# A macaron transformer block: load order, the last output tiles, and an order of steps for every sequence

## The chip, the core and the metric

The kernel runs on one core of one Trainium2 chip. The metric is the device time of one execution in microseconds (us). Before the change the median of three runs is 900.11 us (900.03 to 900.91).

The core has five engines that work side by side, each through its own list of instructions in order: TensorE (PE, with weight loads shown as PEld), VectorE (DVE), ScalarE (ACT), GpSimd (POOL) and SyncE (SP), which here only issues DMA transfers. An instruction waits until the semaphores of what it needs have been raised, and everything behind it on the same engine waits with it. Matmul results go to PSUM, from where VectorE or ScalarE carries them on.

## The reference

Eight sequences of 512 tokens with 256 features pass through half a feed-forward network, attention, and half a feed-forward network again; both feed-forward networks use the same weights.

```python
x = x + 0.5 * ffn(layernorm(x))
x = x + attn(layernorm(x))
x = x + 0.5 * ffn(layernorm(x))

def attn(x, Wq, Wk, Wv, Wo):                # 16 heads of 32 columns
    q, k, v = (heads(x @ W) for W in (Wq, Wk, Wv))
    scores = (q_r @ k_r.T + q_i @ k_i.T) / sqrt(16)
    probs = softmax(where(causal, scores, -inf))
    return concat(probs @ v_r, probs @ v_i) @ Wo

def ffn(x):                                 # 256 -> 1024 -> 256
    h = x @ W_exp + b_exp
    h = butterfly(h, up_weights)            # 10 stages of 2x2 mixing over 1024
    h = gelu(h + up_bias)
    h = butterfly(h, down_weights)
    return h @ W_con + b_con + down_bias
```

A butterfly is linear, so each can be multiplied into the dense matrix beside it once, before any token is touched.

## The kernel before

All arithmetic is in fp32. Matmuls are counted here as the trace shows them, two for each in the source.

**Prologue** (L613 to L632). The up butterfly is folded into W_exp, the down butterfly into W_con. The seven low stages of each are built as one 128x128 matrix per block of 128 features by VectorE (`low_matrices`, L223) and applied by TensorE (`low_up` L252, `low_down` L273). The three high stages pair whole blocks (`high_stage`): ScalarE scales a block (L236; for some of the down stages GpSimd, L238) and VectorE adds the partner (L241). `finish_up` transposes the result into `wup_sb` (L267, copied at L268). Small vectors are needed on the way: the stage coefficients `upc_sb` and `dnc_sb`, the bias `upb_sb`, and `bc_sb` and `db_sb`, which VectorE combines into `bhalf` (L616, L617). GpSimd adds `bhalf` to x (`ffn_bias`, L189). The first sequence's layer norm runs here too: its statistics on VectorE (L154 to L156), its normalization on GpSimd (L172), its transposes on TensorE (L195). `keep_busy` (L259) issues matmuls of the identity into a bank that nobody reads; each counts as two matmuls. The eight steps f of sequence 0 are spread over the down stages, and the statistics and normalization of sequence 1 end the prologue.

**Loads** (L117 to L135). SP and ScalarE each issue into a DMA queue of their own. The tables `upe_sb`, W_exp in two halves with x of sequence 0 between them, `dne_sb`, `wcon_sb`, further x and the attention weights go through SP; five small ones go through ScalarE's queue. A DMA also waits, if need be, until an earlier one on the same completion semaphore has landed; there are eight such semaphores, taken in turn.

**Sequences** (L634 to L636). What follows is one list of steps per sequence, written out as tokens in `ORDER` (L544) and turned into instructions by `sequence` (L573) in just that order: every engine gets its part of each step in the order of the tokens. A number ahead of a token repeats it; `+1`, `-1` and so on name another sequence, relative to the one whose list it is. Sequences 1 to 4 share one list (`None`), the others have their own. The tokens:

| token | step | work |
|---|---|---|
| f, g | `up_steps`, first and second feed-forward network | 4 matmuls of 512 columns (L307), GELU on ScalarE (L314); 8 steps |
| F, G | `down_steps` | 8 matmuls of 256 columns (L325); every fourth step VectorE adds into x (L334), G then stores (L336); 8 steps |
| q, v | `qk_steps`, `v_steps` | 4 matmuls of 512 columns (L350, L368), copy by ScalarE; 8 and 4 steps; q alternates q and k of a head group |
| u0 to u9 | `score_unit` | scores of 4 heads for one or two query blocks (L404) into the one 4-bank PSUM tile; VectorE adds the mask and takes the row maximum (L418), ScalarE exponentiates (L431) |
| t | `turn` | VectorE turns 32x32 blocks of the exponentials (L449, L453) |
| m | `turn_sums`, `move` | VectorE inverts and turns the sums (L458, L459), then SP issues 16 DMAs across partitions (L471) into the one tile `pt` |
| p | `times_v` | probs x V for a head group (L484), scaled by VectorE (L491) |
| w | `wo_steps` | 8 matmuls (L505), VectorE adds into x (L510) every second step |
| s, a, x | layer norm: `ln_stats`, `ln_apply`, `ln_steps`; second letter 1, a, 2 for the first network, attention, the second network | VectorE, rstd on GpSimd (L158), bias addition on GpSimd; x is a write to DRAM and a read back by DMA (L287, L294), which transposes; for three layer norms it is TensorE's transposes instead |
| l | `load_x` | loads x of a later sequence |

Units u0, u1 serve head group 0, u2 groups 0 and 1, u3, u4 group 1, u5, u6 group 2, u7 groups 2 and 3, u8, u9 group 3. Buffers that tie the steps together: PSUM tag `a` has three banks for f, F, g, G, q, v and w; `g` has one buffer; `xnt` two; `pt` one; `e` three; `qt` four and `kt` five.

Of the kernel before, what the change touches and what calls it, by code (L numbers as in the profile page):

```python
# [48 lines left out]
def macaron_kernel(  # L49
# [475 lines left out]
    def attention_steps(b, pool):  # L525
        def moved(g):
# [18 lines left out]
        0: """3F+0 x1+1 F+0 2s1+2 sa+0 F+0 x1+1 3F+0 sa+0 2aa+0 2f+1 2xa+0 a1+2 f+1 q+0 a1+2 q+0 f+1 u0 q+0 v u1  # L545
              2q+0 t0 x1+2 t1b q+0 u2 t1a v t2a f+1 m0 2f+1 u3 f+1 v t2b u4 F+1 t3 F+1 v x1+2 u5 t4a 2F+1 t4b sa+1
              p0 m1 2F+1 aa+1 t5 2F+1 q+0 sa+1 u6 aa+1 q+0 t6b xa+1 u7 xa+1 t6a t7a p1 m2 u8 2q+1 u9 t8 t7b t9b
              2q+1 t9a 3q+1 p2 q+1 m3""",
        None: """u0 5f+1 u1 f+1 t1a 2f+1 u2 t0 p-3 v u3 t2a 3w-1 t1b m0 s2-1 w-1 v s2-1 u4 v 2F+1 a2-1 s1+2 a2-1 F+1
              t3 F+1 t2b x2-1 s1+2 F+1 v u5 t4a p0 t4b 2F+1 x2-1 m1 F+1 g-1 sa+1 4g-1 aa+1 2g-1 t5 sa+1 aa+1 g-1  # L550
              u6 2G-1 u7 p1 G-1 xa+1 t6a xa+1 q+1 t7a t6b m2 G-1 q+1 u8 t7b a1+2 t8 a1+2 q+1 x1+2 G-1 q+1 G-1 u9
              2G-1 x1+2 t9a t9b q+1 p2 q+1 l+3 m3 2q+1""",
        5: """u0 3f+1 s1+2 u1 f+1 s1+2 f+1 u2 t0 f+1 p-3 t1a t1b u3 2w-1 t2a s2-1 2w-1 m0 2f+1 u4 v s2-1 2a2-1 v
              t2b F+1 t4a t3 3F+1 u5 x2-1 a1+2 2v F+1 x2-1 t4b a1+2 u6 x1+2 p0 F+1 m1 F+1 u7 F+1 sa+1 2g-1 sa+1
              aa+1 2g-1 t7a aa+1 g-1 xa+1 t5 t6a 2g-1 xa+1 u8 t6b p1 m2 g-1 G-1 u9 2G-1 q+1 t8 t9b G-1 t7b q+1
              x1+2 q+1 2G-1 t9a p2 m3""",
        6: """u0 q+0 G-2 u1 G-2 f+1 t1b t1a q+0 u2 f+1 t0 q+0 f+1 t2b u3 t2a p-3 m0 q+0 u4 v l+2 t3 w-1 f+1 u5 w-1
              t4b t4a w-1 s2-1 w-1 2v a2-1 v u6 p0 m1 f+1 q+0 3f+1 t6b t6a t5 s2-1 u7 a2-1 3F+1 x2-1 u8 x2-1 F+1
              t7a p1 m2 u9 sa+1 3F+1 t9b F+1 2g-1 sa+1 2aa+1 t9a g-1 xa+1 g-1 t8 g-1 t7b g-1 p2 g-1 xa+1 g-1 m3
              3q+1""",  # L560
# [153 lines left out]
```

## Time and profile before

| what | us | how to read it |
|---|---|---|
| median of 3 runs | 900.11 | 900.03 to 900.91 |
| the profiled execution | 900.17 | its own device time |
| its span | 898.5 | from its first to its last instruction; 1.67 lie around it |
| TensorE busy | 871.0 | overlapping matmuls counted once |
| VectorE busy | 628.8 | |
| ScalarE busy | 516.0 | |
| GpSimd busy | 87.1 | |
| the DMA queue of SP | 129.00 MB | 54.9% of 16 engines' span |
| mean granted TensorE clock | 0.989 | 1 is full speed |

The page's groups that carry most of TensorE's time, and VectorE's and ScalarE's largest (line, engine, operation, shapes and count, then busy us and mean ns, then the idle time before them and what ended it):

```profile
L431 ACT ACTIVATE e<-e,nm 128x128 f32<-128x128 f32 (+3 forms) x512 | 280.3, 549 | 80.1 <-DVE nm L418 79.8
L418 DVE CUSTOM_DVE_ANT_0 e<-sc,mask 128x128 f32<-128x128 f32 (+3 forms) x512 | 216.2, 484 | 141.5 <-PE sc L404 141.4
L325 PE MATMUL py_f<-wdn_sb,g_f 128*128 128x256 f32 x1024 | 233.9, 382 | 0.0
L307 PE MATMUL ph_f<-xnt_f,wup_sb 128*128 128x512 f32 x512 | 229.7, 599 | 2.0 <-ACT g_f L314 2.0
L449 DVE STREAM_TRANSPOSE pr<-e 128x1536 f32<-128x1536 f32 (+2 forms) x128 | 171.2, 1355 | 19.7 <-ACT e L431 19.7
```

The mean of one matmul is its time from start to end; back to back they start closer together. In a timeline, "x8" merges eight like instructions and the bracket at the end gives the idle time of the engine ahead of them and what ended it.

### The profile page before, as it was taken

What the parts mean: (1) busy time and instruction counts of PE and PEld (TensorE: products, weight loads), DVE (VectorE), ACT (ScalarE), POOL (GpSimd) and SP (SyncE); (2) the same over time, 40 slices, a digit from 0 to 9 for tenths busy, and PEclk for the clock granted to TensorE, in tenths of its full rate; (3) what the DMA queues carried; (4) which work ended last, traced back from release to release, by engine and by line L of the source; (5) the groups of instructions that cost most, each with busy time, mean ns of one, the idle gap of its engine ahead of it and who ended that gap; (6) DMA issues with size and microseconds to landing.
All of it is one profiled execution on the core that took longest, in us unless ns stands there. A gap on an engine that the chain in (4) does not pass through costs nothing.

```text
span 898.5 us, 13295 instructions
## 1 busy us (share of the span) xinstructions
PE 871.0 (97%) x4348; PEld 502.6 (56%) x4348; DVE 628.8 (70%) x1812; ACT 516.0 (57%) x1356; POOL 87.1 (10%) x103
## 2 busy tenths in 40 slices
PE   6999979999999999999999999999999999999998
PEld 5574633565645655465554656456564573644656
DVE  6966885685838867397675968589868875888230
ACT  4718746944558364763648445695749764756211
POOL 4230000020100201020010201002000010010010
PEclk8899989999999999999999999999999999999999
DMA  9110667366571657546392665816775577477600
GB/s 327 61 47 24 159 186 174 70 177 175 151 201 44 173 136 210 142 117 171 107 249 62 173 170 128 234 53 171 184 191 131 142 199 195 103 177 192 151 12 23
DMA packets 52931, 130.15 MB, mean 145 GB/s; under 512 B 10880, under 2 KB 32640, under 8 KB 52864
## 3 DMA queue, kind: packets, MB, share of 16 engines
q1 hardware_dynamic: 52144, 129.00, 54.9%
q8 instruction: 34, 0.56, 0.3%
q10 hardware_dynamic: 720, 0.32, 0.2%
q14 instruction: 33, 0.27, 0.1%
HBM read 21.80 MB, written 15.20 MB: 41 GB/s over the span
## 4 chain that ended last, share of the span: by engine, by line
PE 88%; DVE 5%; ACT 3%; SPq 2%; DMA 1%; issue 1%; POOL 0%; DVEq 0%; ACTq 0%; POOLq 0%
PE py_f L325 24%; PE ph_f L307 23%; PE pp L350 10%; PE sc L404 9%; PE pa L484 8%; PE pv L368 6%; PE po L505 6%; SPq L471 2%; DVE e L418 2%; ACT e L431 2%; DMA pt<-pr 1%; DVE high_up L241 1%; PE idle L259 1%; ACT L314 1%; DVE pr L449 1%
## 5 line engine op out<-in xcount | busy, mean ns | idle before, releaser
L431 ACT ACTIVATE e<-e,nm 128x128 f32<-128x128 f32 (+3 forms) x512 | 280.3, 549 | 80.1 <-DVE nm L418 79.8
L418 DVE CUSTOM_DVE_ANT_0 e<-sc,mask 128x128 f32<-128x128 f32 (+3 forms) x512 | 216.2, 484 | 141.5 <-PE sc L404 141.4
L325 PE MATMUL py_f<-wdn_sb,g_f 128*128 128x256 f32 x1024 | 233.9, 382 | 0.0
L307 PE MATMUL ph_f<-xnt_f,wup_sb 128*128 128x512 f32 x512 | 229.7, 599 | 2.0 <-ACT g_f L314 2.0
L325 PEld LDWEIGHTS py_f<-wdn_sb,g_f 128*128 128x128 f32 x1024 | 192.0, 190 | 43.7 <-issue 18.1
L449 DVE STREAM_TRANSPOSE pr<-e 128x1536 f32<-128x1536 f32 (+2 forms) x128 | 171.2, 1355 | 19.7 <-ACT e L431 19.7
L307 PEld LDWEIGHTS ph_f<-xnt_f,wup_sb 128*128 128x128 f32 x512 | 95.7, 191 | 118.8 <-issue 101.4
L314 ACT ACTIVATE g_f<-ph_f,bup_sb 128x512 f32<-128x512 f32 x128 | 84.5, 686 | 130.3 <-PE ph_f L307 130.0
L404 PE MATMUL sc<-kt,qt 32*128 32x128 f32 (+3 forms) x1024 | 92.5, 462 | 5.9 <-ACT kt L357 3.3
L431 ACT ACTIVATION_READ_ACCUMULATOR e<-e,nm 128x1 f32 x512 | 95.7, 187 | 0.0
L484 PE MATMUL pa<-pt,v 128*32 128x512 f32 (+3 forms) x1024 | 77.5, 444 | 5.2 <-DMA td_at<-tx_at 2.2
L404 PEld LDWEIGHTS sc<-kt,qt 32*128 32x128 f32 x1024 | 44.4, 183 | 65.3 <-issue 31.8
L158 POOL TENSOR_TENSOR rstd_f<-mv_f,mhalf 128x2 f32<-128x2 f32 x32 | 22.8, 712 | 479.0 <-DVE mv_f L156 479.0
L484 PEld LDWEIGHTS pa<-pt,v 128*32 128x32 f32 x1024 | 31.4, 111 | 59.9 <-issue 54.2
L350 PE MATMUL pp<-xnt_at,wk_sb 128*128 128x512 f32 x128 | 61.3, 601 | 0.0
L350 PE MATMUL pp<-xnt_at,wq_sb 128*128 128x512 f32 x128 | 61.2, 600 | 0.0
L368 PE MATMUL pv<-wv_sb,xnt_at 128*128 128x512 f32 x128 | 60.7, 603 | 0.0
L505 PE MATMUL po<-wo_sb,ot 128*128 128x256 f32 x256 | 58.7, 384 | 0.1
L334 DVE SCALAR_TENSOR_TENSOR x<-py_f,x 128x512 f32<-128x512 f32 x32 | 21.7, 679 | 52.1 <-PE py_f L325 52.1
L505 PEld LDWEIGHTS po<-wo_sb,ot 128*128 128x128 f32 x256 | 47.7, 190 | 13.3 <-ACT e L431 3.3
L189 POOL TENSOR_TENSOR x<-x,bhalf 128x512 f32<-128x512 f32 x32 | 40.8, 1275 | 145.9 <-DVE xn_f L172 111.4
L357 ACT ACTIVATE kt<-pp 128x512 f32<-128x512 f32 x32 | 18.9, 591 | 46.6 <-PE pp L350 46.6
(74 smaller groups left out, 565.1 us busy)
## 6 DMA issues: line engine op xcount, KB each, us to landing
pt<-pr SPq DMA_DIRECT2D x512, 176.0 KB, 4.1
td_f<-tx_f SPq DMA_DIRECT2D x14, 512.0 KB, 4.7
xnt_f<-td_f SPq DMA_DIRECT2D x56, 128.0 KB, 3.1
x<-in_x_dram SPq DMA_DIRECT2D x8, 512.0 KB, 6.1
out_dram<-x SPq DMA_DIRECT2D x16, 256.0 KB, 4.2
td_at<-tx_at SPq DMA_DIRECT2D x7, 512.0 KB, 4.0
xnt_at<-td_at SPq DMA_DIRECT2D x28, 128.0 KB, 3.0
wexp_sb<-in_wexp_t_dram SPq DMA_DIRECT2D x2, 514.0 KB, 7.3
```

The source lines that it names most:

```text
L189: nc.gpsimd.tensor_tensor(x2, x2, bhalf.rearrange("p (o c) -> p o c", o=1).to_broadcast([P, 2, C]), ALU.add)
L307: nc.tensor.matmul(ph[:, :N], lhsT=wup_sb[:, kc, bass.ts(fc, P)], rhs=xnt[:, :, kc, :].rearrange("p i (t r) -> p t i r", r=32), start=(kc ...
L314: nc.scalar.activation(g[:, fc, :], ph[:, :N], AF.Gelu, bias=bup_sb[:, fc : fc + 1])
L325: nc.tensor.matmul(py[:, i, :], lhsT=g[:, fc, bass.ts(t, P)], rhs=wdn_sb[:, fc, :], start=(fc == 0), stop=(fc == NBLK - 1),)
L350: nc.tensor.matmul(pp[:, :N], lhsT=w[:, kc, bass.ts(g, P)], rhs=xnt[:, :, kc, :], start=(kc == 0), stop=(kc == KC - 1),)
L368: nc.tensor.matmul(pp, lhsT=xnt[:, t, kc, :], rhs=wv_sb[:, kc, :], start=(kc == 0), stop=(kc == KC - 1))
L404: nc.tensor.matmul(sc[:, j, at : at + n], lhsT=kept["q", b, gg][r, bass.ts(qb, P)], rhs=kept["k", b, gg][r, :n], start=(i == 0), stop=True ...
L418: nc.vector.tensor_tensor_reduce(out=e[:, j, at : at + n], in0=sc[:, j, at : at + n], in1=mask[:, N - n :], scale=-1.0, scalar=3.0e38, op0 ...
L431: nc.scalar.activation(e[:, j, at : at + n], e[:, j, at : at + n], AF.Exp, scale=-1.0, bias=nm[:, qb, gg, j : j + 1], accum_out=zs[:, gg, ...
L449: nc.vector.transpose(pr[:, :, :, qb : qb + 3 * n - 2 : 3, :].rearrange("p j h k r -> p h k j r"), blocks[:, :, :n])
L484: nc.tensor.matmul(by_row[r, :, kb * 32 :], lhsT=v[:, kb, bass.ds(g * P + j * HD, HD)], rhs=pt[:, :, bass.ds(j * NSLOT + SLOT[kb] + kb, NT ...
L505: nc.tensor.matmul(po[:, i, :], lhsT=ot[:, g, bass.ts(t, P)], rhs=wo_sb[:, g, :], start=(g == 0), stop=(g == NG - 1))
```

## The change

The loads stand in a hand-written order, with `upc_sb` alone left on ScalarE's queue; `dnc_sb`, `upb_sb`, `bc_sb` and `db_sb` follow `wcon_sb` on SP's. `keep_busy` goes from 26 to 19. `bhalf` and the bias additions of sequence 0 move from ahead of the up fold's end to behind the down stages. For the last sequence, `down_steps` gives each 128-token tile its own PSUM tile, addition and store, where two shared one. `ORDER` has a list for every sequence. The removed rows of `ORDER` are those of L545 to L563 above.

```diff
@@ -115,24 +115,26 @@
     wdn_sb = const.tile([P, NBLK, C], F32, name="wdn_sb")
 
     last = upe_sb.shape[1] - NBLK * P
-    nc.sync.dma_start(out=upe_sb[:, :last], in_=up_e[:, :last])
-    nc.sync.dma_start(out=upe_sb[:, last:], in_=up_e[:, last:])
-    for blocks in (slice(0, NBLK // 2), slice(NBLK // 2, NBLK)):
-        nc.sync.dma_start(out=wexp_sb[:, blocks, :], in_=wexp_t.rearrange("(n p) c -> p n c", p=P)[:, blocks, :])
-        if blocks.start == 0:
-            load_x(0)
-    nc.scalar.dma_start(out=upc_sb, in_=up_c)
-    nc.scalar.dma_start(out=bc_sb, in_=b_con.to_broadcast([P, C]))
-    nc.scalar.dma_start(out=db_sb, in_=dn_b.to_broadcast([P, C]))
-    nc.scalar.dma_start(out=upb_sb, in_=up_b)
-    nc.scalar.dma_start(out=dnc_sb, in_=dn_c)
-    nc.sync.dma_start(out=dne_sb, in_=dn_e)
-    nc.sync.dma_start(out=wcon_sb, in_=wcon.rearrange("(n p) c -> p n c", p=P))
-    load_x(1)
-    for w_sb, w in ((wq_sb, wq), (wk_sb, wk), (wv_sb, wv), (wo_sb, wo)):
-        nc.sync.dma_start(out=w_sb, in_=w.rearrange("(k p) f -> p k f", p=P))
-    for b in range(2, 4):
-        load_x(b)
+    wexp_blocks = wexp_t.rearrange("(n p) c -> p n c", p=P)
+    first, second = slice(0, NBLK // 2), slice(NBLK // 2, NBLK)
+    with tc.manual_schedule():
+        nc.sync.dma_start(out=upe_sb[:, :last], in_=up_e[:, :last])
+        nc.sync.dma_start(out=upe_sb[:, last:], in_=up_e[:, last:])
+        nc.sync.dma_start(out=wexp_sb[:, first, :], in_=wexp_blocks[:, first, :])
+        load_x(0)
+        nc.sync.dma_start(out=wexp_sb[:, second, :], in_=wexp_blocks[:, second, :])
+        nc.scalar.dma_start(out=upc_sb, in_=up_c)
+        nc.sync.dma_start(out=dne_sb, in_=dn_e)
+        nc.sync.dma_start(out=wcon_sb, in_=wcon.rearrange("(n p) c -> p n c", p=P))
+        nc.sync.dma_start(out=dnc_sb, in_=dn_c)
+        nc.sync.dma_start(out=upb_sb, in_=up_b)
+        nc.sync.dma_start(out=bc_sb, in_=b_con.to_broadcast([P, C]))
+        nc.sync.dma_start(out=db_sb, in_=dn_b.to_broadcast([P, C]))
+        load_x(1)
+        for w_sb, w in ((wq_sb, wq), (wk_sb, wk), (wv_sb, wv), (wo_sb, wo)):
+            nc.sync.dma_start(out=w_sb, in_=w.rearrange("(k p) f -> p k f", p=P))
+        for b in range(2, 4):
+            load_x(b)
 
 
     ident = const.tile([P, P], F32, name="ident")
@@ -318,8 +320,10 @@
     def down_steps(b, what, store):
         def step(t, half):
             t2, i = divmod(t, 2)
-            if i == 0 and half == 0:
-                kept["py", what, b] = ps_a.tile([P, 512], F32, name=f"py_{what}_{b}_{t2}", tag="a")
+
+            n = 1 if store and b == B - 1 else 2
+            if i % n == 0 and half == 0:
+                kept["py", what, b] = ps_a.tile([P, 512], F32, name=f"py_{what}_{b}_{t // n}", tag="a")
             g, py = kept["g", what, b], kept["py", what, b].rearrange("p (t c) -> p t c", c=C)
             for fc in range(half * NBLK // 2, (half + 1) * NBLK // 2):
                 nc.tensor.matmul(
@@ -329,12 +333,12 @@
                     start=(fc == 0),
                     stop=(fc == NBLK - 1),
                 )
-            if i == 1 and half == 1:
-                mine = xt[b][:, 2 * t2 : 2 * t2 + 2, :]
-                nc.vector.scalar_tensor_tensor(mine, py, 0.5, mine, ALU.mult, ALU.add)
+            if (i + 1) % n == 0 and half == 1:
+                mine = xt[b][:, t + 1 - n : t + 1, :]
+                nc.vector.scalar_tensor_tensor(mine, py[:, i + 1 - n : i + 1, :], 0.5, mine, ALU.mult, ALU.add)
                 if store:
                     nc.sync.dma_start(
-                        out=out[b, bass.ds(2 * t2 * P, 2 * P), :].rearrange("(t p) c -> p t c", p=P), in_=mine
+                        out=out[b, bass.ds((t + 1 - n) * P, n * P), :].rearrange("(t p) c -> p t c", p=P), in_=mine
                     )
 
         return [partial(step, t, half) for t in range(NT) for half in range(2)]
@@ -542,25 +546,37 @@
 
 
     ORDER = {
...
+        0: """2F+0 s1+2 2F+0 s1+2 F+0 x1+1 2F+0 sa+0 F+0 x1+1 sa+0 2f+1 2aa+0 xa+0 f+1 xa+0 f+1 2q+0 f+1 a1+2 u0
+              q+0 v u1 q+0 v q+0 t0 t1b u2 v t1a t2a f+1 m0 f+1 a1+2 f+1 u3 x1+2 v t2b q+0 u4 3F+1 t3 t4a F+1 u5
+              x1+2 t4b sa+1 F+1 p0 m1 u6 F+1 t5 2F+1 q+0 aa+1 q+0 sa+1 u7 aa+1 f+2 t6a t7a 2f+2 u8 2xa+1 t6b p1 m2
+              t7b 3f+2 q+1 2f+2 q+1 t8 u9 q+1 t9a 2q+1 t9b p2 m3""",
+        1: """u0 q+0 F+1 u1 t0 t1a q+0 2F+1 u2 F+1 q+0 u3 t1b t2a p-3 m0 u4 3w-1 t3 t2b w-1 2v 2s2-1 F+1 2a2-1 F+1
+              x2-1 v u5 t4b v t4a sa+1 2F+1 u6 x2-1 p0 2g-1 sa+1 g-1 aa+1 g-1 t6b 2g-1 aa+1 xa+1 m1 s1+2 t5 g-1
+              t6a g-1 s1+2 G-1 u7 a1+2 G-1 a1+2 G-1 xa+1 x1+2 2G-1 t7a u8 p1 x1+2 m2 u9 t9b G-1 q+1 2G-1 t8 2f+2
+              t9a f+2 t7b q+1 2f+2 p2 f+2 m3""",
+        2: """u0 2q+0 u1 2q+0 t0 l+2 q+0 u2 f+1 q+0 u3 p-3 w-1 t1b t1a w-1 2v f+1 t2a s2-1 s1+2 v m0 t3 u4 a2-1
+              t2b 2w-1 s2-1 F+1 a2-1 v 3F+1 x2-1 t4b F+1 u5 t4a p0 sa+1 x2-1 m1 u6 2F+1 aa+1 F+1 sa+1 t6b 2g-1
+              aa+1 t6a 2g-1 xa+1 g-1 xa+1 g-1 u7 g-1 t5 g-1 a1+2 t7a p1 G-1 s1+2 G-1 m2 G-1 u8 G-1 2q+1 a1+2 u9
+              t9a q+1 x1+2 q+1 t9b t8 2G-1 x1+2 t7b G-1 p2 m3""",
+        3: """u0 G-2 q+0 f+1 2q+0 f+1 u1 f+1 t0 2f+1 u2 p-3 w-1 t1a u3 w-1 t1b v t2b s2-1 2f+1 t2a w-1 m0 u4 w-1 v
+              a2-1 v t3 s2-1 a2-1 l+2 v q+0 f+1 t4a F+1 x2-1 F+1 u5 p0 t4b u6 x2-1 F+1 s1+2 2F+1 m1 u7 F+1 sa+1
+              2F+1 g-1 t6a sa+1 g-1 t7a g-1 t5 t6b 2g-1 s1+2 2aa+1 xa+1 g-1 xa+1 2g-1 u8 p1 m2 u9 t9b G-1 2a1+2
+              x1+2 2G-1 q+1 G-1 t7b q+1 x1+2 q+1 G-1 t8 2G-1 t9a p2 m3""",
+        4: """u0 G-2 2q+0 2f+1 q+0 t0 u1 f+1 q+0 l+2 f+1 u2 p-3 f+1 t1b u3 t1a w-1 v t2a w-1 s2-1 w-1 m0 w-1 a2-1
+              f+1 s2-1 s1+2 a2-1 2f+1 t2b x2-1 v u4 F+1 v 2F+1 t3 t4b t4a F+1 v u5 p0 u6 sa+1 q+0 F+1 x2-1 F+1 m1
+              aa+1 u7 F+1 t6a F+1 g-1 sa+1 t5 2g-1 aa+1 xa+1 5g-1 t6b s1+2 t7a u8 p1 xa+1 m2 u9 q+1 a1+2 t8 q+1
+              2G-1 a1+2 x1+2 2G-1 x1+2 2q+1 t9b q+1 G-1 t9a t7b p2 m3""",
+        5: """u0 3G-2 u1 q+0 t0 t1b q+0 u2 t1a l+2 t2a 3f+1 u3 p-3 v w-1 m0 t2b f+1 s1+2 u4 w-1 s2-1 a2-1 2w-1 v
+              u5 2v s2-1 a2-1 q+0 t3 t4a f+1 x2-1 t4b 2f+1 t5 s1+2 f+1 x2-1 p0 m1 u6 3F+1 a1+2 3F+1 a1+2 F+1 sa+1
+              u7 F+1 sa+1 g-1 x1+2 2aa+1 2g-1 p1 t7a xa+1 g-1 xa+1 2g-1 t6a g-1 t6b g-1 m2 u8 G-1 t8 3G-1 u9 q+1
+              t9a q+1 x1+2 t9b t7b q+1 p2 m3""",
+        6: """u0 q+0 t0 3G-2 u1 q+0 G-2 u2 t1b f+1 t1a q+0 f+1 u3 t2a p-3 m0 u4 w-1 f+1 w-1 s2-1 a2-1 w-1 f+1 w-1
+              v t4a v t4b 2v t2b f+1 t3 s2-1 u5 p0 f+1 m1 f+1 t5 f+1 q+0 a2-1 u6 q+0 F+1 t6b t6a F+1 2x2-1 F+1 u7
+              F+1 t7a p1 m2 u8 F+1 sa+1 2F+1 u9 F+1 g-1 sa+1 2aa+1 3g-1 t8 t7b t9b 2g-1 xa+1 t9a xa+1 p2 m3""",
+        7: """2g-2 3q+0 u0 q+0 u1 2G-2 t0 u2 p-3 t1b t1a G-2 t2a m0 w-1 u3 w-1 G-2 u4 v t2b s2-1 2w-1 t4a t3 a2-1
+              2v s2-1 t4b v p0 m1 q+0 a2-1 q+0 u5 q+0 u6 x2-1 G-2 t5 q+0 t6b u7 t6a t7a x2-1 G-2 p1 m2 G-2 u8 G-2
+              l+1 g-1 t8 2g-1 t7b u9 t9a g-1 t9b 2g-1 p2 m3 2g-1 7G-1 p3 2w+0 s2+0 2w+0 s2+0 G-1 2a2+0 2x2+0 8g+0
+              8G+0""",
     }
     LNS = {"a": "at", "1": "f1", "2": "f2"}
     queues = {}
@@ -571,7 +587,7 @@
         return queues[key, b].pop(0)
 
     def sequence(b, pool):
-        for token in ORDER.get(b, ORDER[None]).split():
+        for token in ORDER[b].split():
             times, rest = (int(token[0]), token[1:]) if token[0].isdigit() else (1, token)
             what, kind, at = rest[0], "", 0
             if what in "sax":
@@ -611,16 +627,14 @@
 
 
     with fold, tc.manual_schedule():
-        keep_busy(26)
+        keep_busy(19)
         mats = low_matrices(upe_sb, "up")
-        nc.vector.tensor_tensor(bhalf, bc_sb, db_sb, ALU.add)
-        nc.vector.tensor_scalar(bhalf, bhalf, 0.5, None, ALU.mult)
         cur = low_up(mats)
         run([partial(ln_stats, 0, "f1", half) for half in range(2)])
         run([partial(ln_apply, 0, "f1", half, nc.gpsimd) for half in range(2)])
         for i in range(HIGH):
             cur, whole = high_stage(cur, i, upc_sb, "up", C + 1, NBLK)
-        run(ln_steps(0, "f1", copy=nc.scalar.copy), partial(ffn_bias, 0, 0), partial(ffn_bias, 0, 1))
+        run(ln_steps(0, "f1", copy=nc.scalar.copy))
         finish_up(cur, whole)
         up = up_steps(0, "f1")
         mats = low_matrices(dne_sb, "dn")
@@ -628,7 +642,10 @@
         for i in range(HIGH - 1, -1, -1):
             cur, _ = high_stage(cur, i, dnc_sb, "dn", C, NBLK if i == HIGH - 1 else NBLK // 2)
             run([up.pop(0) for _ in range(min(3, len(up)))])
+        nc.vector.tensor_tensor(bhalf, bc_sb, db_sb, ALU.add)
+        nc.vector.tensor_scalar(bhalf, bhalf, 0.5, None, ALU.mult)
         low_down(mats, cur)
+        run(partial(ffn_bias, 0, 0), partial(ffn_bias, 0, 1))
         run(lns(1, "f1"))
 
     with tc.tile_pool(name="attn", bufs=1) as attn, tc.manual_schedule():
```

More of the change, by code (lines that the diff above doesn't have):

```diff
@@ L544, in macaron_kernel @@
     ORDER = {
[L545 to L560, printed above, removed]
@@ L561, in macaron_kernel @@
-        7: """u0 q+0 u1 G-2 t0 G-2 u2 p-3 w-1 v t1a G-2 t1b t2a m0 u3 G-2 t2b w-1 u4 s2-1 v t4a w-1 t3 w-1 2v s2-1
-              t4b p0 m1 2a2-1 2q+0 u5 q+0 u6 q+0 x2-1 G-2 t5 t6b u7 t6a G-2 x2-1 t7a p1 m2 G-2 t7b u8 G-2 2g-1 t8
-              g-1 u9 t9b g-1 t9a 2g-1 p2 g-1 m3 g-1 7G-1 p3 2w+0 s2+0 2w+0 s2+0 a2+0 G-1 a2+0 2x2+0 8g+0 8G+0""",
+        0: """2F+0 s1+2 2F+0 s1+2 F+0 x1+1 2F+0 sa+0 F+0 x1+1 sa+0 2f+1 2aa+0 xa+0 f+1 xa+0 f+1 2q+0 f+1 a1+2 u0
+              q+0 v u1 q+0 v q+0 t0 t1b u2 v t1a t2a f+1 m0 f+1 a1+2 f+1 u3 x1+2 v t2b q+0 u4 3F+1 t3 t4a F+1 u5
+              x1+2 t4b sa+1 F+1 p0 m1 u6 F+1 t5 2F+1 q+0 aa+1 q+0 sa+1 u7 aa+1 f+2 t6a t7a 2f+2 u8 2xa+1 t6b p1 m2
+              t7b 3f+2 q+1 2f+2 q+1 t8 u9 q+1 t9a 2q+1 t9b p2 m3""",
```

## The prediction, made before the changed kernel was run

> **What bounds the kernel now.** I read the page first, then TensorE's busy time by stage, then the two stages in which it idles, in order of time.
>
> ```profile
> PE 871.0 (97%) x4348; PEld 502.6 (56%) x4348; DVE 628.8 (70%) x1812; ACT 516.0 (57%) x1356; POOL 87.1 (10%) x103
> PEclk8899989999999999999999999999999999999999
> ```
>
> TensorE is the bound. No matmul is added or removed, so a new order can only win what PE idles, what it loses at a low clock, and its switching costs. By stage (busy us of PE, PEld, DVE, ACT, POOL, then granted clock):
>
> ```profile
> 0.00:25.00 25.00, 16.67 (x82) 13.85 (x83) 17.26 (x40) 11.85 (x27) 10.99 (x18) 0.85 0.97 330
> 60.00:153.04 93.04, 86.80 (x416) 42.32 (x415) 69.57 (x201) 57.72 (x162) 4.65 (x5) 0.96 0.47 119
> 153.04:258.49 105.45, 104.95 (x529) 60.04 (x528) 74.69 (x221) 60.91 (x163) 9.24 (x10) 1.00 0.60 157
> 790.00:850.00 60.00, 56.19 (x302) 31.83 (x300) 38.67 (x102) 30.22 (x81) 3.22 (x3) 1.00 0.70 178
> ```
>
> The idle time lies in the start (8.3), sequence 0 (6.2) and sequence 7 (3.8); sequences 1 to 4 idle 0.5 each. TensorE's timeline shows the kinds of wait:
>
> ```profile
> 120.81 0.71 PE L404 MATMUL sc<-kt,qt 32*128 32x256 f32 x8 [1.05 <-DVE nm L418]
> 123.14 0.96 PE L404 MATMUL sc<-kt,qt 32*128 32x256 f32 x8 [1.62 <-ACT kt L357]
> 126.26 4.33 PE L484 MATMUL pa<-pt,v 128*32 128x512 f32 x32 [2.15 <-DMA td_at<-tx_at]
> 146.83 2.36 PE L484 MATMUL pa<-pt,v 128*32 128x512 f32 x32 [1.38 <-DMA pt<-pr]
> 263.47 3.70 PE L307 MATMUL ph_f<-xnt_f,wup_sb 128*128 128x512 f32 x8 [0.50 <-ACT g_f L314]
> 800.82 1.99 PE L350 MATMUL pp<-xnt_at,wq_sb 128*128 128x512 f32 x4
> 803.55 1.15 PE L404 MATMUL sc<-kt,qt 32*128 32x384 f32 x16 [0.74 <-DVE nm L418]
> ```
>
> Brackets hold the idle time and its releaser. First kind: a score unit (u) reuses the PSUM tile that VectorE is still reading. Second: q/k must be copied by ScalarE, behind a unit's exponentials. Third: probs x V (p) waits for the transfer of its move (m). Fourth: GELU tiles queue behind exponentials.
>
> The start, in the timeline and in L241's windows (busy and count of VectorE):
>
> ```profile
> 10.30 1.91 PE L252 MATMUL low_up<-wexp_sb,mat_up 128*128 128x257 f32 x8
> 12.25 2.67 ACT L236 ACTIVATE mine_up<-low_up,upc_sb 128x257 f32<-128x257 f32 x7 [5.80 <-PE low_up L252]
> 19.71 2.67 POOL L189 TENSOR_TENSOR x<-x,bhalf 128x512 f32<-128x512 f32 x2
> 13.85:19.66 5.81, 5.81 (x14) 0.83 1.07 387
> 19.66:22.77 3.11, 3.01 (x4) 0.50 1.06 377
> 22.77:26.10 3.33, 3.26 (x8) 0.50 1.08 342
> ```
>
> Fourteen L241 steps start in 5.81 us, two in the next 3.11 (the other two counted only touch its edges), eight in the last 3.33. The slow pair lies under POOL's bias additions.
>
> **The change, part by part.** All against the profiled execution: 900.17 us, its span 898.5 and 1.67 around it; the median of the runs is 900.11.
>
> *1. Start.* upe's second half lands at 6.95 and W_exp's first at 9.49, 2.5 apart; full 0.5 MB loads behind them land 1.4 apart (10.87, 12.32). The difference goes to the small loads from ScalarE's queue. Without them W_exp would land near 7.8, x near 9.2 (now 10.87), W_exp's second half near 10.6 (now 12.32). The matrices are done at 8.28. keep_busy: 27 matmuls start by 7.4, 0.213 apart, then every 0.111; 38 instead of 52 end near 8.7. So low_up starts at 8.7, not 10.3; its first half takes 1.75, ScalarE starts near 10.6 instead of 12.25, and L241 near 12.2 instead of 13.85: **-1.65**. Taking bhalf (0.42 + 0.29) from there saves nothing, as VectorE waited for x anyway. Then the bias additions leave POOL: the slow pair costs 0.8 instead of 3.11: **-2.3**. TensorE's clock is 0.5 from 17.7 to 27.9, 4.6 us after the transposes at 23.31 began; they would begin near 19.3 and the next change on that grid is near 24.5, so ph_f loses **+0.25**. Sum -3.7. Bounds: no gain from the loads and a cold low_up (1.75 more) leave about -0.5; -4.2 at best.
>
> A rule speaks against the shorter warm-up. The Trainium skill, TensorE: Matmul & The Clock Gate (Part 1: The HAM clock gate), says that the clock rises after a busy window of about 3.4 us that runs free of the program. By it, an unlucky phase would keep all 38 cold and low_up too; the trace's own change at 7.4 is the lucky case. By the rule's worst case the sum would be about 3 us higher.
>
> What is moved costs nothing if its cover holds. Four small loads now precede x_1 and the weights in SP's queue, at 0.34 to 0.5 us per issue about 1.8 us, against transfers that start 1.75 us sooner; x_1 lands at 18.85 and is first used at 42.66. dnc lands near 16 and is used near 23. bhalf and two bias additions (2 x 1.27) now precede sequence 1's statistics and rstd: its transposed copy, complete near 56.0, comes 1.7 later, against a first use at 58.97; 1.2 us stay. If that cover is gone, f+1 waits up to 1.5.
>
> *2. Sequence 0.* Idle of 1.05, 1.62, 2.15 and 1.38; the stall also halves the clock until 130.3, and pa takes 4.27 instead of 2.29. Sum 8.2. Between u6 and u7 stood one q (1.8 us, against VectorE's 2.8); now F, 2F, two q, 8.8 us. For p, the chain of waits gives the transfer's length:
>
> ```profile
> 131.55 0.72 DVE pr L459
> 132.34 0.51 SPq L471
> 141.47 4.71 DMA pt<-pr
> 146.83 2.36 PE pa L484 x32
> ```
>
> From the sums' end at 132.26 to the last landing near 146.5 is 14.3: sixteen issues, then the last flight. I compare it with the PE work between m and p, by rows: u 1.07, p 2.29, q/v/f/g 1.72, F/G/w 1.73, 0.1 for each change between kinds. Before, sequence 0 had 13.0 for group 1 and 14.6 for group 2, whose sums also came 1.4 late: the two waits. Now 17.6 and 18.6. I leave 0.7 for new waits: k of group 3 is made directly ahead of u7 (0.2), and x_1's transposed copy is due as q+1 starts (0.5). **-7.5**; bounds -4 (one stall stays, with its clock) and -8.2.
>
> *3. GELU waits.* Sequences 1 to 4 began u0 5f, and f fills three PSUM buffers before ScalarE is through its exponentials and table load. None begins so now: **-2.0**.
>
> *4. New waits.* Eight times only a p now lies between two units: sequences 1 and 3 (u3/u8, u5/u8), 4 (u5, u8), 2 (u5), 6 (u3). The rows of 800.82 and 803.55 show 2.73 us from the first matmul after a unit to the next unit, all VectorE's minimum pass; p takes 2.29. 8 x 0.44 = **+3.5**. Bounds: 0, if the pass has slack I don't see; 8 x (0.44 + 1.36), one turn of L449 standing ahead each time, 14.4. I take the near row.
>
> *5. Sequence 7.* Waits of p0 (0.60) and p3 (0.30) go: their gaps grow from 14.7 and 13.9 to 18.1 and 15.7. Its q-after-u waits stay. m0 moves ahead of VectorE's lag: +0.4. **-0.5**. G moved ahead of both normalizations near 862 is worth nothing, within 0.5 either way: VectorE has the same work.
>
> *6. Switches.* Reading the orders, PE changes kind 192 times instead of 202, at 0.1 each: **-0.9**.
>
> *7. End.* After the last matmul VectorE adds 128x256 instead of 128x512: 0.42 (the bias addition of that size) for 0.69. The final store halves: between nothing and 1.1 (128 KB copies land in 3.1, 256 KB stores in 4.2); I take 0.25. **-0.5**. The extra additions fall on an idle VectorE.
>
> Sum: -3.7 - 7.5 - 2.0 + 3.5 - 0.5 - 0.9 - 0.5 = -11.6. 900.2 - 11.6 = **888.6**.
>
> **Rivals.** *The head start is hidden* (14 in 100): sequence 1's late copy, or a cold clock, takes it all; only parts 2 to 7 count, 892.3. For: 1.2 us of cover. Against: the copy's chain starts as much sooner as the rest.
>
> *VectorE a turn behind at each of the eight places* (7): +10.9, 899.5, hardly a change. For: several intervals have more VectorE than PE work. Against: the intervals ahead of these are long (14 us of PE against 10 before sequence 2's u5), so the backlog is gone.
>
> *Slower: late transfers* (10). SP issues in order, and a read of a transposed copy waits for its write to land, up to 4.6 us; if m stands behind it, the 14.3 grows. Over the new gaps (smallest 14.3, 14.6, 14.7, 15.7) the shortfall sums to 1.4 us at 15, 11.2 at 17, 21.8 at 18, 37 at 19. It eats the whole gain from about 17.1; at 18 the time is 910. For: sequence 0 has a transfer of 16.0. Against: issues followed the sums by 0.1, and nearly all transfers took 13.9 to 15.2.
>
> **How the numbers follow.** The forecast has 69 in 100. Its own range is about 884.5 to 893. The range 884.5 to 896.5 adds the first rival and leaves out the other two and 3 of the forecast's tails: 20 in all. This measurement can't tell 0.2% (1.8 us) from no change. Faster: 69 + 14 + 1 of the second rival = 84; the same 4; slower 12.
>
> **What would show it.** Right: low_up near 8.7, the transposes near 19.3, no wide PE gap in 115 to 150, no GELU wait of 0.5, PE gaps of 0.3 to 0.5 ahead of scores that follow a p, a last VectorE step of 0.4. Wrong: PE gaps ahead of pa released by DMA, a clock of 0.5 past the first 30 us, or gaps ahead of scores well over 1 us.

## The result, and the profile after

| | before | changed |
|---|---|---|
| median, us | 900.43 (4 runs, 900.03 to 900.91) | 885.77 (4 runs, 884.92 to 887.00) |
| ratio | 1 | 0.9838, 95% interval 0.9821 to 0.9855 |
| profiled execution, its span | 900.17, 898.5 | 884.92, 883.1 |
| PE idle between its first and last matmul | 21.96 | 16.20 |

The change saves 14.7 us; the prediction said 11.6 (888.6, range 884.5 to 896.5). The profiled execution is the shortest of the four, 0.85 under the median. Page of the changed kernel, busy time and the clock row:

```profile
PE 862.1 (98%) x4334; PEld 499.9 (57%) x4334; DVE 628.0 (71%) x1814; ACT 520.1 (59%) x1360; POOL 87.1 (10%) x103
PEclk8999999999999999999999999999999999999999
```

PE has 14 fewer instructions, the warm-up matmuls. Of the three 8s that the clock row had before, two are gone, the one at sequence 0 (sixth digit) among them. The same stretches of time as before (busy us of PE, PEld, DVE, ACT, POOL, then the granted clock, DMA share and GB/s):

```profile
0.00:25.00 25.00, 18.59 (x82) 15.06 (x83) 17.46 (x46) 14.54 (x34) 8.54 (x17) 0.86 0.97 328
60.00:153.04 93.04, 92.97 (x452) 46.12 (x451) 67.66 (x197) 65.97 (x175) 3.93 (x4) 1.00 0.48 125
790.00:850.00 60.00, 56.48 (x319) 36.24 (x311) 33.43 (x92) 25.72 (x71) 2.07 (x3) 1.00 0.59 149
```

Sequence 0 idles 0.07 instead of 6.2 and keeps its clock. The last row holds other work than before, since all of it comes about 14 us sooner; like against like, five waits of sequence 7 (ahead of p 0, of p 2 and of three score units) make 3.8, as before. The start of the changed kernel, in its timelines:

```profile
8.34 1.91 PE L254 MATMUL low_up<-wexp_sb,mat_up 128*128 128x257 f32 x8
10.28 2.67 ACT L238 ACTIVATE mine_up<-low_up,upc_sb 128x257 f32<-128x257 f32 x7 [4.12 <-PE low_up L254]
15.03 6.95 DVE L243 SCALAR_TENSOR_TENSOR high_up<-high_up,upc_sb,mine_up 128x257 f32<-128x257 f32 x16
19.27 4.22 PE L269 MATMUL pup<-ident,high_up 128*128 128x128 f32 x16
```

The first two rows stood at 10.30 and 12.25, and the transposes in the last at 23.31. The sixteen VectorE steps of the third row took 9.03 from 17.00 while GpSimd added the bias; now no addition lies beside them. TensorE's timeline further on:

```profile
123.17 2.36 PE L488 MATMUL pa<-pt,v 128*32 128x512 f32 x32
144.39 2.36 PE L488 MATMUL pa<-pt,v 128*32 128x512 f32 x32
...
291.85 1.15 PE L408 MATMUL sc<-kt,qt 32*128 32x384 f32 x16 [0.36 <-DVE nm L422]
...
476.84 1.55 PE L309 MATMUL ph_f<-xnt_f,wup_sb 128*128 128x512 f32 x3 [0.71 <-ACT v L375]
...
779.08 2.36 PE L488 MATMUL pa<-pt,v 128*32 128x512 f32 x32 [0.79 <-DMA out_dram<-x]
...
789.55 1.15 PE L408 MATMUL sc<-kt,qt 32*128 32x384 f32 x16 [0.74 <-DVE nm L422]
```

The two p of sequence 0 have no bracket: no wait. The third row is one of eight waits of 0.36 to 0.37 behind a p that stands alone between two units (166, 220, 291, 391, 422, 499, 528, 671): foreseen. The fourth is new and was not foreseen: in sequence 4 ScalarE's copy of v stands behind a table load (1.28) and the exponentials of u3. The last two are waits of sequence 7 that stayed; the fifth row is that of p 0 (its bracket names a store, whose landing counts on the same semaphore as one of the sixteen transfers; the last of these landed at 778.62). The end:

```profile
876.95 0.42 DVE L338 SCALAR_TENSOR_TENSOR x<-py_f,x 128x256 f32<-128x256 f32 x1 [3.45 <-PE py_f L329]
877.40 3.36 SPq L340 DMA_DIRECT2D out_dram<-x  x2
879.98 0.42 DVE L338 SCALAR_TENSOR_TENSOR x<-py_f,x 128x256 f32<-128x256 f32 x1 [2.61 <-PE py_f L329]
```

Of each tile only 0.42 of VectorE and a 128 KB store follow the last matmul; from there to the end of the span it is 3.19 instead of 3.87.

### The profile page after: what moved, and what is told of

It reads as the page before. It is cut to its first block, busy times and chain, and to the rows that moved or that the text cites. A ratio compares the mean times of both kernels' runs of the same rounds, so it can differ in the third digit from the quotient of the medians.

```text
span 883.1 us, 13289 instructions
## 1 busy us (share of the span) xinstructions
PE 862.1 (98%) x4334; PEld 499.9 (57%) x4334; DVE 628.0 (71%) x1814; ACT 520.1 (59%) x1360; POOL 87.1 (10%) x103
## 4 chain that ended last, share of the span: by engine, by line
PE 84%; DVE 8%; ACT 3%; DMA 2%; SPq 1%; issue 1%; POOL 0%; DVEq 0%; ACTq 0%; POOLq 0%
PE py_f L329 23%; PE ph_f L309 23%; PE pp L354 12%; PE sc L408 9%; PE pa L488 6%; PE pv L372 5%; PE po L509 5%; DVE e L422 4%; ACT e L435 2%; SPq L475 1%; DVE pr L453 1%; DVE high_up L243 1%; PE idle L261 1%; DMA td_f<-tx_f 1%; PE pup L269 0%
## 5 line engine op out<-in xcount | busy, mean ns | idle before, releaser
L488 PE MATMUL pa<-pt,v 128*32 128x512 f32 (+3 forms) x1024 | 75.6, 435 | 1.8 <-issue 1.0
L338 DVE SCALAR_TENSOR_TENSOR x<-py_f,x 128x512 f32<-128x512 f32 (+1 forms) x34 | 22.2, 652 | 55.2 <-PE py_f L329 55.2
```

The costliest lines, as they stand in the source:

```text
L488: nc.tensor.matmul(by_row[r, :, kb * 32 :], lhsT=v[:, kb, bass.ds(g * P + j * HD, HD)], rhs=pt[:, :, bass.ds(j * NSLOT + SLOT[kb] + kb, NT ...
```

## The experiments

Every ratio is against runs of the kernel before on the same chip (medians 900.31 to 900.63). The table cuts each profiled span into five stretches: to the first F step; from there to p of group 3 of sequence 7 ("p3"); from p3 to the first up matmul of the last tail; the 32 up matmuls; and from the first down matmul behind them to the end of the span.

| kernel | to F | F to p3 | p3 to up | up | down to end |
|---|---|---|---|---|---|
| before | 45.00 | 805.57 | 15.47 | 14.59 | 17.85 |
| start alone (e1_start) | 41.00 | 804.36 | 15.33 | 13.84 | 18.06 |
| orders alone (e2_order) | 46.17 | 795.87 | 15.75 | 14.80 | 18.05 |
| last tiles alone (e3_tiles) | 45.13 | 805.03 | 15.33 | 15.23 | 17.16 |
| changed | 40.84 | 795.67 | 15.61 | 13.84 | 17.16 |
| changed, again (e0_after) | 40.74 | 795.73 | 15.61 | 15.53 | 17.16 |

Each part moves its own stretch, and the whole is the parts side by side. One column belongs to none of them: the up matmuls took 13.84 in one profile of the changed kernel and 15.53 in another. One stretch is free of scatter: from the first F step to u1 of sequence 7 (750.15 in the changed kernel, behind a wait of 0.74) it takes 709.30 or 709.31 in all eight profiles that have the lists of the changed kernel up to there, e2_order's with the old start too; before it took 719.00.

**The three parts, each alone in the kernel before.** e1_start takes the hunks of the loads and of the prologue, e2_order the lists, e3_tiles `down_steps`.

> Kernel before with the start alone changed (order of the loads, 19 instead of 26 keep-busy pairs, bias late). Theory: what the start gains passes through, since everything behind it waits for TensorE: 4.1 us faster than before (the changed kernel's first down-projection matmul came 4.15 us sooner), and with the old order sequence 0 keeps its waits of 1.0 to 2.2 us. Rival: the head start is eaten by the first wait for the transposed copy or by sequence 0's waits: 0 to 1.5 us faster.

> Kernel before with the new lists of steps alone. Theory: the order earns its part by itself: 10 to 10.7 us faster (9.9 between the first down projection and the last probs x V, 0.6 in the last layer norm), with eight gaps of 0.37 us ahead of scores that follow a probs x V. Rival: the lists fit only the earlier start: 8 us or less, with new gaps in sequence 0.

> Kernel before with only the last sequence's tiles added and stored one by one. Theory: 0.5 to 0.75 us faster, 0.27 of it in the last addition, the rest in the smaller last store. Rival: a store's time does not depend on its size here: 0.3 us.

Measured: e1_start 895.64, ratio 0.9943 (0.9931 to 0.9956), 5.0 faster; of these 4.0 lie ahead of the first F step, and 1.2 in sequence 0, whose low clock lasted 3.4 instead of 6.8 us in that profile. e2_order 892.77, 0.9911 (0.9896 to 0.9926), 7.9 faster: by time a miss, at the rival's 8 and not at the theory's 10. Its profile speaks for the theory: between F and p3 it saves 9.7, with the eight gaps of 0.37 and none new in sequence 0 above 0.05; it gives back 1.2 in a start whose clock was low from 20.09 to 30.33 instead of 17.66 to 27.90, and 0.7 behind p3, where the theory had a gain of 0.6. e3_tiles 899.97, 0.9996 (0.9987 to 1.0004): by time inconclusive; by its profile the last stretch is 0.69 shorter. The sum of the three, 13.5, agrees with the 14.7 of the whole inside the intervals. The start is not hidden, so the first rival falls.

**The bias additions alone (e4_bias).** In the kernel before:

```diff
-        nc.vector.tensor_tensor(bhalf, bc_sb, db_sb, ALU.add)
-        nc.vector.tensor_scalar(bhalf, bhalf, 0.5, None, ALU.mult)
-        run(ln_steps(0, "f1", copy=nc.scalar.copy), partial(ffn_bias, 0, 0), partial(ffn_bias, 0, 1))
+        run(ln_steps(0, "f1", copy=nc.scalar.copy))
...
+        nc.vector.tensor_tensor(bhalf, bc_sb, db_sb, ALU.add)
+        nc.vector.tensor_scalar(bhalf, bhalf, 0.5, None, ALU.mult)
         low_down(mats, cur)
+        run(partial(ffn_bias, 0, 0), partial(ffn_bias, 0, 1))
```

> Kernel before with only bhalf and sequence 0's bias additions moved behind the down stages; loads and 26 keep-busy pairs as before. Theory: the two VectorE steps that took 1.5 us each beside GpSimd's additions take 0.4: 2.3 us faster. Rival: the additions were not what slowed them, or the start is bound by the loads: 0 to 0.5 us.

Measured: 897.32, 0.9965 (0.9953 to 0.9978), 3.1 faster in the runs (interval 2.0 to 4.2, which holds the theory's 2.3); in the profile the first F step stands at 43.12 instead of 45.00, 1.9 sooner. VectorE's timeline of this kernel:

```profile
17.21 7.07 DVE L241 SCALAR_TENSOR_TENSOR high_up<-high_up,upc_sb,mine_up 128x257 f32<-128x257 f32 x16
```

The sixteen steps take 7.07, not 9.03. About 2 of the 4 us of the start come from taking 2.67 us of GpSimd's work away from beside VectorE.

**The warm-up, longer and much shorter (e5_busy26, e6_busy8), beside the changed kernel itself (e0_after).**

```diff
-        keep_busy(19)
+        keep_busy(26)
```

```diff
-        keep_busy(19)
+        keep_busy(8)
```

> The changed kernel as it is, beside the three variants of it in the same rounds: 14.5 us faster than before, as in its first runs.

> The changed kernel with 26 keep-busy pairs again. Theory: the pairs end near 9.9 instead of 8.3 and the whole start follows: 1.3 to 1.6 us slower than the changed kernel. Rival: the start is bound by the loads of W_exp and x, which now land at 7.5 to 10.4: at most 0.3 us slower. Second rival: the longer warm-up keeps the clock up for the fold: faster.

> The changed kernel with keep_busy(8) instead of keep_busy(19): 16 warm-up matmuls, which end at 5.1 instead of 8.3. Theory (the warm-up buys the clock): the granted clock is still low when the fold begins at about 8.0, the fold's first eight matmuls take some 3.5 us instead of 1.9, and the first F step of sequence 0 starts 0.8 to 2 us later than 40.8. Rival (the fold waits for the tables on VectorE and the second half of W_exp, so a cold clock is hidden there, and the shorter warm-up lets it begin 0.3 earlier): the first F step at 40.4 to 41.0, the time the same within the measurement.

Measured: e0_after 886.35, 0.9846 (0.9833 to 0.9860). With 26, 888.12, 0.9871 (0.9857 to 0.9884), the first F step at 42.23 instead of 40.74. With 8, 888.40, 0.9868 (0.9855 to 0.9882), and 42.18. TensorE's timeline with 26:

```profile
1.67 8.55 PE L261 MATMUL idle<-ident 128*128 128x128 f32 x52 [1.67 <-POOL ident masks.py:199]
10.06 3.21 PE L254 MATMUL low_up<-wexp_sb,mat_up 128*128 128x257 f32 x14
```

and with 8, its timeline:

```profile
1.67 3.58 PE L261 MATMUL idle<-ident 128*128 128x128 f32 x16 [1.67 <-POOL ident masks.py:199]
7.89 4.99 PE L254 MATMUL low_up<-wexp_sb,mat_up 128*128 128x257 f32 x14 [2.65 <-DVE mat_up L225]
```

With 26 the warm-up itself holds the fold back to 10.06. With 8 the fold could begin at 7.89, as soon as its matrices are there, but PE had idled 2.65 us, the clock fell to 0.5 from 8.31 to 11.73, and fourteen matmuls took 4.99 instead of 3.21. The eight profiles with 19 have their first F step between 40.74 and 41.73, so 19 is between two losses of 0.45 to 1.5. The medians of 26 and 8 lie 1.8 and 2.0 over e0_after's; all runs with 26, but not all with 8, are above all runs of the changed kernel. The warm-up buys the clock, as the theory had it.

**Fillers between u and p (e7_fill).** Six of the eight lone p's get one step of F, G or q ahead of them, taken from a group of such steps behind, as here in sequence 2:

```diff
-              t2b 2w-1 s2-1 F+1 a2-1 v 3F+1 x2-1 t4b F+1 u5 t4a p0 sa+1 x2-1 m1 u6 2F+1 aa+1 F+1 sa+1 t6b 2g-1
+              t2b 2w-1 s2-1 F+1 a2-1 v 3F+1 x2-1 t4b F+1 u5 F+1 t4a p0 sa+1 x2-1 m1 u6 F+1 aa+1 F+1 sa+1 t6b 2g-1
```

> The changed kernel with one F, G or q moved between score unit and probs x V at six of the eight places where a probs x V alone lies between two units. Theory: six waits of 0.37 (0.44 with the drain that they hide) go, and six more runs of full-width matmuls cost 0.2 each: 1.2 to 1.6 us faster than the changed kernel, two gaps of 0.37 left. Rival: the added switches cost as much as the waits: no difference.

Measured: 885.78, 0.9832 (0.9817 to 0.9847): too near e0_after for the time to tell. By the profile F to p3 takes 794.49, 1.24 less; up to u1 of sequence 7, where no scatter is, 708.06 instead of 709.31. TensorE's timeline at the place of the 291.85 row above:

```profile
289.71 1.99 PE L329 MATMUL py_f<-wdn_sb,g_f 128*128 128x256 f32 x8
291.63 2.36 PE L488 MATMUL pa<-pt,v 128*32 128x512 f32 x32
293.92 1.15 PE L408 MATMUL sc<-kt,qt 32*128 32x384 f32 x16
```

All six waits are gone: 6 x 0.365 idle, and 6 x 0.07 since a p that is followed at once takes 2.29 and not 2.36, make 2.6. A new gap of 0.08 comes in, which costs 0.15 (in e11_best below it is absent, and the stretch takes 707.90). So 1.2 of the gain went into six more runs of full-width matmuls, 0.2 each. The starts of the matmuls say the same: the last 512-column matmul of a full-width run and the narrow one behind it start 0.52 apart, not 0.43, and the first two of a run start 0.10 further apart than the others. This prices a switch: the prediction's 0.1 for each change of kind is half of it.

**The last layer norm's bias (e8_latebias, e10_onebias).** In the last layer norm of the changed kernel the fourth normalization on VectorE took 1.36, the other three 0.41 each. e8_latebias issues the two GpSimd additions behind both normalizations; e10_onebias makes them one instruction over all four tiles.

```diff
-            ffn_bias(b, half)
+            if (b, what) == (B - 1, "f2"):
+                if half == 1:
+                    run(partial(ffn_bias, b, 0), partial(ffn_bias, b, 1))
+            else:
+                ffn_bias(b, half)
```

```diff
-            ffn_bias(b, half)
+            if (b, what) != (B - 1, "f2"):
+                ffn_bias(b, half)
+            elif half == 1:
+                x4 = xt[b][:, :, :]
+                nc.gpsimd.tensor_tensor(
+                    x4, x4, bhalf.rearrange("p (o c) -> p o c", o=1).to_broadcast([P, NT, C]), ALU.add
+                )
```

> The changed kernel with GpSimd's bias additions of the last layer norm behind both its normalizations. Theory: VectorE's four normalizing steps take 1.5 instead of 2.3 us, so TensorE's gaps of 1.5 and 0.9 near 848 shrink by 0.8: 0.8 us faster than the changed kernel. Rival: those gaps are set by rstd and the statistics: no difference.

> The changed kernel, with the last layer norm's two bias additions on GpSimd made one instruction over all four token tiles, which can start only when the fourth normalization has read x. Theory (the GpSimd addition that begins at 849.45 stretches the fourth normalization on VectorE from 0.41 to 1.36 us, and TensorE waits 0.94 for it): that normalization takes 0.41, the 0.94 gap closes, and from p of group 3 of sequence 7 to the first up matmul of the last tail takes 14.6 to 14.8 instead of 15.61; the span is 0.9 shorter at the same clock. Rival (the stretch comes from something else, or the longer addition stretches VectorE's two copies of the transposed rows instead): 15.4 to 15.7, nothing gained.

Measured: e8_latebias 885.70, 0.9841 (0.9828 to 0.9855); e10_onebias 885.10, 0.9834 (0.9821 to 0.9848). The timeline of the changed kernel:

```profile
848.03 0.69 DVE L338 SCALAR_TENSOR_TENSOR x<-py_f,x 128x512 f32<-128x512 f32 x1
848.64 2.32 DVE L174 TENSOR_SCALAR xn_f<-x,mv_f,rstd_f 128x256 f32<-128x256 f32 x4
849.45 1.36 POOL L191 TENSOR_TENSOR x<-x,bhalf 128x512 f32<-128x512 f32 x1 [0.36 <-DVE xn_f L174]
851.02 0.77 PE L197 MATMUL pxt_f<-ident,xn_f 128*128 128x128 f32 x5 [0.94 <-DVE xn_f L174]
```

of e8_latebias:

```profile
848.78 2.32 DVE L174 TENSOR_SCALAR xn_f<-x,mv_f,rstd_f 128x256 f32<-128x256 f32 x4
849.59 1.36 POOL L195 TENSOR_TENSOR x<-x,bhalf 128x512 f32<-128x512 f32 x1 [0.37 <-DVE xn_f L174]
```

and of e10_onebias:

```profile
849.68 1.37 DVE L174 TENSOR_SCALAR xn_f<-x,mv_f,rstd_f 128x256 f32<-128x256 f32 x4
850.23 1.65 PE L203 MATMUL pxt_f<-ident,xn_f 128*128 128x128 f32 x8 [1.48 <-DVE xn_f L174]
851.13 2.35 POOL L190 TENSOR_TENSOR x<-x,bhalf 128x1024 f32<-128x1024 f32 x1 [1.01 <-DVE xn_f L174]
```

e8_latebias tested nothing. GpSimd had no other work, so its addition still began as soon as the first two tiles had been read, 0.81 behind the first normalization as before: the place in the list does not hold an instruction back, only what it reads and writes does. e10_onebias does hold it back. The four normalizations then take 1.37 instead of 2.32, all eight transposes run without a gap, and p3 to the first up matmul is 14.67 instead of 15.61. The wait of 1.48 ahead of them stays, so it is not the additions'; and VectorE's two copies beside the longer addition take 0.69 and 0.68, as before, so the rival falls. That GpSimd stretches VectorE's step is shown by the profile; the time of 0.9 is below what the runs tell. The Trainium skill, SBUF — State Buffer (SBUF: two separate sides), says that VectorE and GpSimd share a port pair that one of them holds for a whole instruction. The rows agree: the fourth normalization begins at 849.60, 0.15 after GpSimd's addition, and ends at 850.96, 0.15 after it.

**One filler ahead of p 0 of sequence 7 (e12_q).**

```diff
-              2v s2-1 t4b v p0 m1 q+0 a2-1 q+0 u5 q+0 u6 x2-1 G-2 t5 q+0 t6b u7 t6a t7a x2-1 G-2 p1 m2 G-2 u8 G-2
+              2v s2-1 t4b v q+0 p0 m1 a2-1 q+0 u5 q+0 u6 x2-1 G-2 t5 q+0 t6b u7 t6a t7a x2-1 G-2 p1 m2 G-2 u8 G-2
```

> The changed kernel, with one q step of sequence 7 moved from behind p of group 0 to ahead of it (1.72 us of TensorE work). Theory (in sequence 7 the chain p, scaling of its result on VectorE, sums of the next group, 14.1 us of transfer, next p sets the pace, so a wait that is filled comes back at the next p): the wait of 0.79 ahead of p 0 is gone, p 0 starts 0.9 to 1.1 later against its landing, a wait of about 1 us stands ahead of p 1 where there is none now, and p of group 3 starts within 0.3 of 795.7 after the first F step. Rival, as the prediction's term for sequence 7 had it (each wait stands by itself and its cover is counted from the place of m): the wait goes and nothing comes back, so 794.8.

One run, 887.28, its up matmuls at a low clock (16.31), so only the profile counts: F to p3 is 795.07. TensorE's timeline:

```profile
780.26 2.36 PE L488 MATMUL pa<-pt,v 128*32 128x512 f32 x32
...
798.75 0.64 PE L488 MATMUL pa<-pt,v 128*32 128x512 f32 x4 [0.65 <-DMA pt<-pr]
```

The wait of 0.79 ahead of p 0 is gone, and one of 0.65 stands ahead of p 1, where there was none: so far the theory holds, p 0 sets when the next group's sums are taken and so when its transfer lands. But the waits ahead of p 2 and p 3 fell (the first gone, the second 0.43 to 0.09; a gap of 0.46 came in behind p 2), and 0.66 of the stretch was gained, nearer the rival's 0.9 than the theory's 0.3. The transfers scatter here: from u1 of sequence 7 to p 3 it takes 86.35 to 87.03 in the nine other profiles with the new lists, and 85.76 in e12_q, so 0.6 is the least that was gained, by this one profile. The sums of m2 were not bound to p 1: in the changed kernel VectorE's turns from 799.54 for 2.90 us hold back the scaling of p 1's result (802.37, though p 1 was through at 800.93), and in e12_q those turns began 0.5 sooner. Of the pace in sequence 7, p 0 to p 1 goes by the transfer and p 1 to p 2 by VectorE's queue; both theories were half right.

**Both gains together (e11_best).** The edits of e7_fill and e10_onebias.

> The changed kernel with six fillers between u and p, and the last bias addition in one piece. Theory: the two gains add up, 1.24 in the sequences (seen between the first F step and p of group 3 of sequence 7: 794.49 instead of 795.73) and 0.9 in the last layer norm, so 2.1 under the changed kernel: 883.6 to 884.2 where the changed kernel has 886.0. Rival (the additive part in the last layer norm is only moved on): 884.7 to 885.2.

Measured: 884.90, 0.9819 (0.9806 to 0.9833). From the first F step to the end of the span it takes 841.80, against 844.04 in e0_after, both with a stretch of low clock in the up matmuls (15.53): 2.24 less, where 2.1 was expected. Its start was 1.0 later in that profile. By time alone it lies in the rival's range (884.7 to 885.2). Its median is 1.4 under e0_after's and 0.9 under the changed kernel's first runs; the intervals overlap, so that it beats the changed kernel rests on the profile.

## Why the prediction was right, and where it was off

Against the profiled execution before, the spans differ by 15.3; the rows below add up to 15.4. "Overlap" is what a stall breaks besides its idle time. Back to back, 512-column matmuls start 0.43 apart and one alone takes 0.59, so 0.16 goes at a stall between full-width matmuls, and the first two behind it start 0.10 further apart as well; between narrow and full-width ones it is 0.07.

| step of the sum | predicted | measured | from |
|---|---|---|---|
| 1 start | -3.7 | -4.15 | first F step 45.00 to 40.84 |
| 2 sequence 0 | -7.5 | -8.6 | idle 6.2, low clock 2.2, overlap 0.6; two small new waits +0.4 |
| 3 GELU waits | -2.0 | -3.1 | 4 x (0.50 idle + 0.16 + 0.10) |
| 4 new waits u-p-u | +3.5 | +3.5 | 8 x (0.365 + 0.07) |
| a wait for v in sequence 4 | none | +1.0 | 0.71 idle + 0.16 + 0.10 |
| waits of w for VectorE, before | none | -0.9 | three of 0.2 inside the overlap, one of 0.3 |
| 5 sequence 7 | -0.5 | +0.15 | p0 0.60 to 0.79, p2 0.76 to 0.58, p3 0.30 to 0.43 |
| 5 order in the last layer norm | 0 | +0.14 | p3 to up 15.47 to 15.61 |
| 6 switches | -0.9 | -2.0 | 10 x 0.2 |
| the clock in the last up matmuls | none | -0.75 | 14.59 to 13.84 |
| 7 end | -0.5 | -0.7 | last stretch 17.85 to 17.16 |

The mechanisms of the large terms held, and the sum was 3.1 short of the 14.7 measured; 885.77 lies 1.3 above the lower end of the range. It fell short mainly by sizes: stalls without their overlap, and the switches. The -0.75 of the clock is luck: in e0_after the same stretch took 15.53, 0.94 more than before.

1. *Start.* The mechanism was right: low_up at 8.34 (8.7 foreseen), the transposes at 19.27 (19.3). Of the two gains, the additions off GpSimd gave 2.1 (9.03 to 6.95; 2.3 foreseen), and the loads with the shorter warm-up 2.0 (1.65). These two belong together: with the new loads and 26 pairs low_up still began at 10.06 (e5_busy26), against 10.30 before; with the old loads W_exp's first half landed only at 9.49, now at 7.45. The clock was low from 16.81 to 23.63. The cover of the moved bias held: TensorE has no gap between 41 and 116. The prediction's rule on the clock, by which an unlucky phase keeps the whole warm-up cold, did not strike at 19: in all eight profiles with 19 the clock rose between 4.6 and 7.8, and low_up ran at full clock. So the rise at 7.4, which the prediction took for the lucky case, is a late one. The loss at 8 pairs is another: there the clock had risen at 4.90 and fell at 8.31, after the idle stretch behind the warm-up.
2. *Sequence 0.* Right; of the 0.7 left for new waits 0.4 was spent, and each stall had cost more than its idle time.
3. *GELU waits.* Right, short of the overlap, 0.26 at each.
4. *New waits.* Right to 0.1. The second rival (VectorE a turn behind) would have shown eight gaps of 1.7.
5. *Sequence 7.* This step failed. It counted the cover from the place of m; but the sums that start the transfer stand on VectorE behind the scaling of the p before, or behind other turns, so a filler between m and p may start the transfer later as well. Ahead of p 0 it counted 18.1 from the place of m0, which TensorE passed at 760.08; VectorE turned the sums only from 763.41 to 764.12, so 14.2 were left, against a transfer of 14.5. Timelines of the changed kernel:

```profile
760.08 1.89 PE L509 MATMUL po<-wo_sb,ot 128*128 128x256 f32 x8
759.75 3.48 DVE L453 STREAM_TRANSPOSE pr<-e 128x512 f32<-128x512 f32 x3
763.41 0.71 DVE L463 STREAM_TRANSPOSE pr<-zr 128x512 f32<-128x512 f32 x1
```

   The waits ahead of p 0 and p 3, which were to go, stand in all nine profiles with this list (0.44 to 1.06 and 0.20 to 1.20); the 0.15 of the table is inside this scatter. The last layer norm's order cost a little: with the old order at full clock (e1_start) p3 to up is 15.33, now 15.61, within the 0.5 that was said.
6. *Switches.* Mis-sized. The count was right: the trace has ten fewer runs of full-width matmuls between F and p3 (90 to 80). Each is worth 0.2 (e7_fill), not 0.1. What else the stretch gained, 0.9, are waits that the prediction did not see, three of the four without a gap between matmuls: in the lists of sequences 2, 3, 4 and 7 the weight load of a w step waited for the result that VectorE scales. TensorE's weight loads before, one of the four:

```profile
281.37 1.81 PEld L505 LDWEIGHTS po<-wo_sb,ot 128*128 128x128 f32 x9 [0.33 <-DVE ot L491]
```

7. *End.* Right.

The slower rival (late transfers) does not occur: from the sums' end to the last landing it takes 13.9 to 15.6 over all groups, against 13.9 to 16.0 before.

## What to carry to other kernels

Price a stall at its idle time and the overlap that it breaks, and a switch between narrow and full-width matmuls by a pair of profiles that differ in the number of runs. Before filling a wait, follow the chain of what it waits for back to the engine's queue: where that chain begins at the step that is delayed, the wait can come back one step later, as ahead of p 1 in e12_q. Moving an instruction in an engine's list delays it only if something stands ahead of it; to hold it back, make it depend on what must be first.

## What was not expected of the hardware

The changed kernel and its repetition are one program, and their up matmuls in the last tail took 14.00 and 15.70. Windows of TensorE around it, for the changed kernel (busy us, count, granted clock, then DMA share and GB/s):

```profile
846.24:849.66 3.42, 1.94 (x9) 1.00 0.00 1
849.66:853.07 3.41, 2.12 (x9) 1.00 0.22 75
853.07:856.48 3.41, 3.41 (x9) 1.00 0.00 0
```

and for e0_after:

```profile
845.75:849.16 3.41, 1.93 (x10) 1.00 0.00 0
849.16:852.57 3.41, 2.12 (x9) 1.00 0.23 77
852.57:855.99 3.42, 3.42 (x5) 0.50 0.00 0
```

In every profile the clock changes lie whole multiples of 3.413 us apart (here cut on that grid), at a phase that differs from run to run: its first rise came between 4.6 and 7.9 us. This agrees with the free-running window of the Trainium skill, TensorE: Matmul & The Clock Gate (Part 1: The HAM clock gate). But how busy a window must be is not settled by these: the first warm-up matmul starts at 1.67, so the rise at 4.6 (e11_best) had at most 2.9 us of matmuls before it; and the same 2.12 of 3.41 kept the clock in one of the profiles above and lost it in the other. It makes 1.7 us between two runs of one kernel, more than six of the eleven terms above, and is why differences under a microsecond had to be read from stretches of the profile and not from times.
